# First convolution kernels wholly on VectorE, lengths and later chunks tied behind them, and sixteen products of ones ahead of the first strip

## The chip, the cores and the metric

The kernel runs on one core of a Trainium2 chip. The metric is the device time of one execution in microseconds (us), as the median of several runs. A core has five engines with a queue each: TensorE (PE in the profile, with its weight loads as PEld), VectorE (DVE), ScalarE (ACT), GpSimd (POOL) and SyncE (SP), whose queue issues most transfers here. Each engine takes its instructions strictly in the order in which the program has them, and waits on semaphores for the others.

## The reference

`x` is 128 x 32 x 512 (batch, head, position). Each head has a causal convolution kernel of 512 taps, made of 64 complex exponentials; the convolution's output is cut at each row's length, goes through a mixture of 16 experts with 4 chosen per row and one shared expert, and is added to `x`.

```python
dtA = A * dt[:, None]
Ct = Cc * (jnp.exp(dtA) - 1.0) / A
P = dtA[:, :, None] * jnp.arange(length)
K = 2.0 * jnp.einsum('hn,hnl->hl', Ct, jnp.exp(P)).real
...
y = irfft(rfft(u, n) * rfft(K, n))[..., :L] + u * D[:, None]
y = y * mask[:, None, :]            # position < length of the batch row
...
scores = sigmoid(y @ gate_w.T) + bias
topk_w, topk_idx = top_k(scores, 4) # weights divided by their sum
out = sum over chosen experts of w * (silu(y @ Wg.T) * (y @ Wu.T)) @ Wd.T
out = out + silu(y @ Sg.T) * (y @ Su.T) @ Sd.T
x = x + out
```

## The kernel before

The work runs in four stages on one core. First the **prologue** makes the first convolution kernels. Then the **convolution** handles 32 heads, four at a time (`NB` = 8 groups of `HB` = 4): for each head, `convolve` makes four products with the head's input `xt` as weights and a Toeplitz strip as moving data (512, 384, 256 and 128 columns; a float32 product is two instructions in the trace), multiplies the result by the length mask on VectorE (`yb`, L527), turns it with four transposes against the permutation `to_rank` (`pt`, L530) and copies it to `yT` (L531). `gates` and `route` compute the gate for each group and each pair of groups. Third comes the **shared expert** over all rows in eight units, and last the **chosen experts**, tile by tile, up to the end.

Convolution kernels come in chunks of pairs of heads. `CHUNKS` is `((0, 2), (2, 4), (6, 4), (10, 6))`: start and number of pairs; a pair of heads is one column of 128 partitions. For a chunk, `waves` forms angle and exponent with two interleaved chains on VectorE (the angle in `wr`, `wk`, the exponent in `wv`, `we`, `wq`, `ws`; the magnitude is `wm`), with two sines on ScalarE, and one outer product (`wv`, L309) on GpSimd. `kernels` then multiplies: the real halves (`f_r`, `ge_r`, `gg_r`, `gg_i`) on VectorE, the imaginary ones (`f_i`, `ge_i`, `gg_t`) on GpSimd. TensorE contracts them (`pk`, L394), VectorE adds the skip term (`krow`, L402), and SyncE writes the row to memory (`kd`) and reads it back as 128 shifted copies (`kernel_strip`, L419). The first chunk carries 16 further columns through the same waves for the factor `Ct` (`em`, `er`, `ei`, `nr`, `ni`, `rd`, `ct_r`, `ct_i`). Of the first group, each head's strip is a transfer of its own; of later groups, all four are one.

Between the first chunk and the loop, the program handles the lengths: keys (`key_row`, `key_col`, `num_len`, `longer`), two counting products (`rank_ps`), the permutations `to_rank` and `to_row`, then `by_rank`, `reach`, `k_u`, `unit_rows` for the shared expert, and the mask `within`. Nothing ties them to a place.

A scheduler orders each engine's queue from the program's order and its own idea of durations, so that program order and queue order differ: in the kernel before, many lengths instructions stand among those of the first chunk on VectorE, and so does the beginning of the second chunk. `chunk_at` says behind which head the later chunks are made. A manual dependence (`tc.add_manual_dep`) makes the scheduler put one instruction behind another.

Of the kernel before, what the change touches and what calls it, by code (L numbers as in the profile page):

```python
# [40 lines left out]
E, TOPK, I = 16, 4, 256  # L41
KT = L // P
IT = I // P
HB = 4
NB = H // HB
RB = 2
UB = 16
NU = B // UB
TU = UB * H
# [5 lines left out]
ONE_HOTS = 8  # L55
AHEAD = 4
# [14 lines left out]
LA, LB = 32, 16  # L71
# [4 lines left out]
def ssm_moe_kernel(  # L76
# [15 lines left out]
    nc = tc.nc  # L92
# [34 lines left out]
    nc.gpsimd.memset(dsk, 0.0)  # L127
# [21 lines left out]
    def load_xt(tb):  # L149
        t = xp.tile([P, KT, HB, P], F32, tag="x", name=f"xt{tb}")  # L150
        nc.sync.dma_start(out=t, in_=x_t[tb])
        return t

# [69 lines left out]
    nc.gpsimd.memset(run_on, 1.0)  # L223
    nc.gpsimd.memset(run_on[:, :, 0:1], 0.0)

    run_e = const.tile([P, RB * HB, E], F32, tag="run_e", name="run_e")
    nc.gpsimd.memset(run_e, 1.0)
    nc.gpsimd.memset(run_e[:, :, 0:1], 0.0)

    def floor_div(out_, in_, by):  # L230

        nc.vector.tensor_scalar(
            out_, in_, 1.0 / by, -(by - 1) / (2.0 * by), ALU.mult, ALU.add
        )
        nc.vector.tensor_scalar(out_, out_, ROUND, None, ALU.add)
        nc.vector.tensor_scalar(out_, out_, ROUND, None, ALU.subtract)

# [35 lines left out]
    CHUNKS = ((0, 2), (2, 4), (6, 4), (10, 6))  # L273
# [16 lines left out]
    nc.gpsimd.memset(f_r, 0.0)  # L290
    nc.gpsimd.memset(f_i, 0.0)
# [3 lines left out]
    def waves(c0, n, lead):  # L295


        w = lead + n * NX
        v, r, k, q = (wide(t, w) for t in ("wv", "wr", "wk", "wq"))
        s, mag = wide("ws", w, I32), wide("wm", w)  # L300

        def pairs(t):
            return t[:, lead:].rearrange("p (c x) -> p c x", x=NX)

        by_l = lab.unsqueeze(1).to_broadcast([P, n, NX])
        nc.vector.tensor_mul(
            pairs(r), by_l, dta_i[:, c0 : c0 + n].unsqueeze(2).to_broadcast([P, n, NX])
        )
        nc.gpsimd.tensor_mul(  # L309
            pairs(v), by_l, dta_r[:, c0 : c0 + n].unsqueeze(2).to_broadcast([P, n, NX])  # L310
        )
        if lead:
            nc.vector.tensor_copy(r[:, :lead], dta_i)
            nc.vector.tensor_copy(v[:, :lead], dta_r)
        reduce_angle(r, k)
        nc.vector.scalar_tensor_tensor(k, r, -1.0, r, ALU.mult, ALU.max)
        nc.scalar.activation(k, k, AF.Sin, bias=half_pi, scale=-1.0)
        half = None
        if lead:
            half = ptile("half")  # L320
# [28 lines left out]
    nc.gpsimd.tensor_mul(m0, nar, nar)  # L349
    nc.gpsimd.tensor_mul(m1, aim, aim)  # L350
    nc.gpsimd.tensor_add(m0, m0, m1)
# [15 lines left out]
    def kernels(c0, n, mag, cos, sin):  # L367

        cs = slice(c0, c0 + n)

        for j in range(2):
            rows = slice(j * N, (j + 1) * N)
            nc.vector.tensor_mul(f_r[rows, cs, j, :], cos[rows, :, LA:], mag[rows, :, LA:])
            nc.gpsimd.tensor_mul(f_i[rows, cs, j, :], sin[rows, :, LA:], mag[rows, :, LA:])
# [7 lines left out]
        nc.gpsimd.tensor_mul(e_i, sin[:, :, :LA], mag[:, :, :LA])  # L382
# [3 lines left out]
        nc.gpsimd.tensor_mul(g_t, e_i, by_i)  # L386
        nc.vector.tensor_add(g_r, g_r, g_t)
        nc.vector.tensor_mul(g_i, e_r, by_i)
        nc.gpsimd.tensor_mul(e_i, e_i, by_r)
# [12 lines left out]
        nc.vector.tensor_add(  # L402
# [7 lines left out]
        for h in range(2 * c0, 2 * (c0 + n)):  # L410
            kd_of[h] = kd[h - 2 * c0 : h - 2 * c0 + 1, :]

# [11 lines left out]

    kernels(*CHUNKS[0], *first)
    kernel_strip(0)


    len_col = const.tile([P, 1], F32, tag="len_col", name="len_col")
    nc.vector.tensor_copy(len_col, len_col_i)  # L430
    key_row = const.tile([P, B], F32, tag="key_row", name="key_row")
    nc.vector.tensor_copy(key_row, len_row_i)
    key_col = const.tile([P, 1], F32, tag="key_col", name="key_col")
    for key, raw, own in ((key_row, key_row, cpos), (key_col, len_col, ppos)):
        nc.vector.tensor_scalar(key, raw, 0.0, float(L), ALU.max, ALU.min)
        if key is key_col:
            num_len = const.tile([P, 2], F16, tag="num_len", name="num_len")
            nc.vector.tensor_copy(num_len[:, 0:1], ppos)
            nc.vector.tensor_copy(num_len[:, 1:2], key)
        nc.vector.scalar_tensor_tensor(key, key, float(P), own, ALU.mult, ALU.subtract)  # L440
# [14 lines left out]
    to_rank_h = const.tile([P, P], F16, tag="to_rank_h", name="to_rank_h")  # L455
    nc.vector.tensor_copy(to_rank_h, to_rank)

    by_rank_ps = ps_m.tile([P, 2], F32, tag="m", name="by_rank_ps")
    nc.tensor.matmul(by_rank_ps, lhsT=to_rank_h, rhs=num_len, start=True, stop=True)
    by_rank = const.tile([P, 2], F32, tag="by_rank", name="by_rank")  # L460
    nc.vector.tensor_copy(by_rank, by_rank_ps)


    reach = const.tile([P, KT], BF16, tag="reach", name="reach")
    nc.vector.memset(reach, 1.0)
    for n in range(1, KT):
        nc.vector.tensor_scalar(
            reach[:, n : n + 1], by_rank[:, 1:2], float(n * P), None, ALU.is_gt
        )

    unit = const.tile([P, NU], BF16, tag="unit", name="unit")
    nc.vector.tensor_scalar(unit, upos, 0.0, None, ALU.is_equal)
    reach_sum = const.tile([P, 1], F32, tag="reach_sum", name="reach_sum")
    nc.vector.tensor_reduce(reach_sum, reach, AX.X, ALU.add)
    reach_b = const.tile([P, 1], BF16, tag="reach_b", name="reach_b")
    nc.vector.tensor_copy(reach_b, reach_sum)
    k_u_ps = ps_m.tile([1, NU], F32, tag="m", name="k_u_ps")
    nc.tensor.matmul(k_u_ps, lhsT=reach_b, rhs=unit, start=True, stop=True)
    k_u = const.tile([1, NU], I32, tag="k_u", name="k_u")
    nc.vector.tensor_copy(k_u, k_u_ps)  # L480


    div = const.tile([P, 2], F32, tag="div", name="div")
    mod = const.tile([P, 1], F32, tag="mod", name="mod")
    floor_div(div[:, 0:1], rank, UB)
    floor_div(div[:, 1:2], ppos, UB)
    nc.vector.scalar_tensor_tensor(mod, div[:, 0:1], -float(UB), rank, ALU.mult, ALU.add)
    same_mod = const.tile([P, P], F16, tag="same_mod", name="same_mod")
    nc.vector.tensor_scalar(same_mod, pmod, mod, None, ALU.is_equal)
    row_u = const.tile([P, NU], F16, tag="row_u", name="row_u")  # L490
    nc.vector.tensor_scalar(
        row_u, cpos[:, :NU], div[:, 0:1], ppos, ALU.is_equal, ALU.mult
    )
    row_ps = ps_m.tile([P, NU], F32, tag="m", name="row_ps")
    nc.tensor.matmul(row_ps, lhsT=same_mod, rhs=row_u, start=True, stop=True)
    part = const.tile([P, TU // P], F32, tag="part", name="part")
    nc.vector.tensor_scalar(
        part, cpos[:, : TU // P], float(P // UB), div[:, 1:2], ALU.mult, ALU.add
    )
    unit_rows = const.tile([P, NU, TU // P], I32, tag="unit_rows", name="unit_rows")  # L500
    nc.vector.scalar_tensor_tensor(
        unit_rows,
        row_ps.unsqueeze(2).to_broadcast([P, NU, TU // P]),
        float(H),
        part.unsqueeze(1).to_broadcast([P, NU, TU // P]),
        ALU.mult,
        ALU.add,
    )
# [3 lines left out]
    nc.vector.tensor_scalar(within, lpos, len_col, None, ALU.is_lt)  # L512
# [337 lines left out]

    def dep(of, on, why):
        tc.add_manual_dep(of.ins, on.ins.name, SYNC, reason=why)
# [345 lines left out]
```

## Time and profile before

| what | value |
|---|---|
| time, median of 3 runs | 957.14 us (956.81 to 957.47) |
| the profiled execution | 961.51 us, of which the span is 959.8 us |
| TensorE busy | 890.6 us, 93% of the span |
| VectorE busy | 427.6 us, 45% |
| GpSimd busy | 432.0 us, 45% |
| ScalarE busy | 171.3 us, 18% |
| chain that ended last | TensorE 78%, VectorE 15%, issue 3% |
| first convolution product starts | 27.09 us |

The span runs from the first to the last instruction; the profiled execution is a single one and stands 4.4 us above the median of the other three. In the chain of waits one goes back from the last instruction to whatever released each step; a stage in which that chain is on one engine is bound by it. A start-to-start distance between two neighbouring rows of the timeline says what an instruction costs its queue, which can be less than its duration, because neighbours that do not depend on each other overlap.

### The profile page before, as it was taken

How to read it: one execution, taken by the hardware profiler on the slowest of the kernel's cores; microseconds unless marked ns; L12 is line 12 of the kernel's file. 1: busy time of each engine (PE TensorE's matmuls, PEld its weight loads, DVE VectorE, ACT ScalarE, POOL GpSimd, SP SyncE). 2: the span in 40 equal slices, each digit the busy share in tenths (PEclk: the TensorE clock that was granted, in tenths of full speed). 3: DMA queues.
4: the chain of work that ended last, by engine and by line, in shares of the span. 5: the costliest groups of instructions: out<-in, count | busy, mean ns of one | idle time of the engine just before them, and what ended most of it. 6: DMA issues, size and time to landing. Idle time of an engine off the chain costs nothing.

```text
span 959.8 us, 14544 instructions
## 1 busy us (share of the span) xinstructions
PE 890.6 (93%) x2960; PEld 443.3 (46%) x2960; DVE 427.6 (45%) x1438; ACT 171.3 (18%) x343; POOL 432.0 (45%) x400
## 2 busy tenths in 40 slices
PE   0799994989998999999999999999999999999995
PEld 0455652344444444444444444444444544444442
DVE  7955555868762233443334233423433323334332
ACT  1122221000001012221222122212222112222211
POOL 4210002033456545664556455655555445556644
PEclk9999997989999999999999999999999999999998
DMA  4467732164456676687667766766666646677755
GB/s 161 126 228 265 233 125 68 66 223 151 165 193 196 251 166 111 127 138 164 113 119 140 166 109 120 137 108 106 125 121 114 112 90 113 112 119 138 131 110 104
DMA packets 54032, 135.94 MB, mean 142 GB/s; under 512 B 12784, under 2 KB 12944, under 8 KB 51344
## 3 DMA queue, kind: packets, MB, share of 16 engines
q0 software_dynamic: 35616, 89.77, 47.5%
q1 hardware_dynamic: 14064, 36.15, 11.4%
q10 hardware_dynamic: 4224, 8.39, 2.3%
q8 instruction: 71, 1.16, 0.5%
q14 instruction: 57, 0.47, 0.1%
HBM read 288.08 MB, written 52.25 MB: 355 GB/s over the span
## 4 chain that ended last, share of the span: by engine, by line
PE 78%; DVE 15%; issue 3%; another core or an unknown queue 1%; DMA 1%; POOL 1%; ACT 0%; SPq 0%; DVEq 0%; POOLq 0%; ACTq 0%
PE g L1044 33%; PE o L1070 24%; PE m L1012 4%; PE o L930 3%; PE u L1062 3%; PE py L520 3%; PE u L904 2%; DVE cols L794 2%; PE g L904 2%; DVE rows L793 1%; DVE yb L527 1%; PE pt L530 1%; DVE wq L261 1%; PE parts L549 1%
## 5 line engine op out<-in xcount | busy, mean ns | idle before, releaser
L1044 PE MATMUL g<-store,yt 128*128 x742 | 343.1, 596 | 4.1 <-ACT yt L1018 2.7
L1080 POOL DMA_INDIRECT out<-xg,put x134 | 212.1, 1583 | 236.5 <-DVE junk L1019 203.2
L1070 PE MATMUL o<-store,zT 128*128 x536 | 252.2, 593 | 1.3 <-DVE zT L1065 1.3
L1056 DVE SCALAR_TENSOR_TENSOR zt<-g,wt,sgt 128x256 f32<-128x256 f32 x135 | 65.3, 483 | 287.0 <-ACT sgt L1055 272.6
L1044 PEld LDWEIGHTS g<-store,yt 128*128 128x128 f32 x742 | 130.3, 190 | 121.0 <-issue 116.8
L1070 PEld LDWEIGHTS o<-store,zT 128*128 128x128 f32 x536 | 101.3, 190 | 130.5 <-issue 124.3
L869 POOL DMA_INDIRECT yg<-y_rows,get x140 | 138.8, 991 | 42.8 <-issue 30.2
L1079 DVE COPY xg<-o 128x512 f32<-128x512 f32 x134 | 92.7, 692 | 110.3 <-PE o L1070 109.4
L1018 ACT COPY yt<-m 128x512 f32<-128x512 f32 x136 | 79.6, 586 | 238.1 <-PE m L1012 225.9
L1055 ACT ACTIVATE sgt<-g 128x256 f32<-128x256 f32 x135 | 51.9, 384 | 268.6 <-PE g L1044 227.8
L1012 PEld LDWEIGHTS m<-ident,yg 128*128 128x128 f32 x373 | 48.5, 141 | 73.2 <-issue 73.0
L520 PE MATMUL py<-strip,xt 128*128 128x512 f32 (+3 forms) x256 | 77.7, 443 | 5.0 <-DMA strip<-kd 5.0
L918 POOL DMA_INDIRECT xg<-in_x,unit_rows x32 | 31.1, 970 | 108.9 <-DVE sig_k L255 99.5
L939 POOL DMA_INDIRECT out<-xg,unit_rows x32 | 31.5, 984 | 98.6 <-DVE xg L937 90.4
L930 PE MATMUL o<-store,z 128*128 128x512 f32 x128 | 60.5, 622 | 6.1 <-DVE xg L937 6.1
L1012 PE MATMUL m<-ident,yg 128*128 128x128 f32 x373 | 63.3, 273 | 1.1 <-issue 1.1
L1065 DVE COPY zT<-u 128x256 f32<-128x256 f32 x134 | 56.3, 420 | 0.1
L520 PEld LDWEIGHTS py<-strip,xt 128*128 128x128 f32 x256 | 41.9, 194 | 21.8 <-issue 9.3
L1062 PE MATMUL u<-ident,zt 128*128 128x128 f32 x268 | 51.2, 273 | 0.0
L904 PE MATMUL g<-store 128*128 128x512 f32 x92 | 44.5, 621 | 0.7 <-ACT store L531 0.7
L904 PE MATMUL u<-store 128*128 128x512 f32 x92 | 42.9, 601 | 0.8 <-issue 0.8
L930 PEld LDWEIGHTS o<-store,z 128*128 128x128 f32 x128 | 24.8, 199 | 38.0 <-issue 28.0
(272 smaller groups left out, 519.7 us busy)
## 6 DMA issues: line engine op xcount, KB each, us to landing
store<-in_w_all SPq DMA_DIRECT2D x143, 1536.0 KB
xt<-in_x_t SPq DMA_DIRECT2D x8, 1024.0 KB
y_rows<-yb ACTq DMA_DIRECT2D x8, 1024.0 KB
strip<-kd SPq DMA_DIRECT2D x7, 1024.0 KB
yg<-y_rows,get POOLq DMA_INDIRECT x140
out<-xg,put POOLq DMA_INDIRECT x134
strip<-kd SPq DMA_DIRECT2D x4, 256.0 KB
xg<-in_x,unit_rows POOLq DMA_INDIRECT x32
```

The costliest lines, as they stand in the source:

```text
L520: nc.tensor.matmul(py[:, : L - jt * P], lhsT=xt[:, jt, q, :], rhs=strip[tb][:, q, jt * P :], start=(jt == 0), stop=(jt == KT - 1),)
L869: nc.gpsimd.indirect_dma_start(out=at(yg, t), out_offset=None, in_=y_rows[:, :], in_offset=bass.IndirectOffsetOnAxis(ap=made["get"][:, t : ...
L904: nc.tensor.matmul(ps[it], lhsT=w_sh[:, c0 : c0 + P], rhs=yT[:, u, kt, :, :].rearrange("p h b -> p (h b)"), start=(kt == KT - n), stop=(kt ...
L930: nc.tensor.matmul(po, lhsT=at(zu, u)[:, it, q * P : (q + 1) * P], rhs=w_sh[:, c0 : c0 + L], start=(it == 0), stop=(it == IT - 1),)
L1012: nc.tensor.transpose(pt[:, q, :], at(yg, t)[:, q * P : (q + 1) * P], ident)
L1018: nc.scalar.copy(at(yt, t), pt)
L1044: mm = nc.tensor.matmul(pgu, lhsT=at(yt, t)[:, q, :], rhs=ring_flat[:, bass.ds(w0s[t] + q * 2 * I, 2 * I)], start=(q == KT - n), stop=(q = ...
L1056: nc.vector.scalar_tensor_tensor(at(zs, t), pgu[:, I:], at(wts, t), sg, ALU.mult, ALU.mult)
L1062: nc.tensor.transpose(at(p_z, t)[:, it, :], at(zs, t)[:, it * P : (it + 1) * P], ident)
L1070: mm = nc.tensor.matmul(po, lhsT=at(zts, t)[:, it, :], rhs=ring_flat[:, bass.ds(w0s[t] + WD + it * L, L)], start=(it == 0), stop=(it == IT ...
L1079: nc.vector.tensor_copy(ob, po)
L1080: add = nc.gpsimd.indirect_dma_start(out=out, out_offset=bass.IndirectOffsetOnAxis(ap=put[:, t : t + 1], axis=0), in_=ob, in_offset=None, ...
```

## The change

Seven memory fills move from GpSimd to VectorE (`dsk`, two of `run_on`, two of `run_e`, `f_r`, `f_i`). In the first chunk all that GpSimd did goes to VectorE (`wv`, `m0`, `m1`, `f_i`, `ge_i`, `gg_t`). A new `behind` ties instructions behind the first chunk's `krow` addition: the lengths' first ones, `within`, and the first products of each later chunk. What the shared expert needs of the lengths moves into a function `ranks`, called before the third group of heads. The chunks become 2, 2, 4 and 8 pairs, the last one made behind head 7 instead of head 5. `keep_warm` adds sixteen products of a 128 x 128 matrix of ones with itself, repeated to 512 columns; nothing reads their result.

```diff
-    nc.gpsimd.memset(dsk, 0.0)
+    nc.vector.memset(dsk, 0.0)
...
-    nc.gpsimd.memset(run_on, 1.0)
-    nc.gpsimd.memset(run_on[:, :, 0:1], 0.0)
+    nc.vector.memset(run_on, 1.0)
+    nc.vector.memset(run_on[:, :, 0:1], 0.0)
...
-    nc.gpsimd.memset(run_e, 1.0)
-    nc.gpsimd.memset(run_e[:, :, 0:1], 0.0)
+    nc.vector.memset(run_e, 1.0)
+    nc.vector.memset(run_e[:, :, 0:1], 0.0)
...
-    CHUNKS = ((0, 2), (2, 4), (6, 4), (10, 6))
+    CHUNKS = ((0, 2), (2, 2), (4, 4), (8, 8))
...
-    nc.gpsimd.memset(f_r, 0.0)
-    nc.gpsimd.memset(f_i, 0.0)
+    nc.vector.memset(f_r, 0.0)
+    nc.vector.memset(f_i, 0.0)
...
-        nc.vector.tensor_mul(
+        first_op = nc.vector.tensor_mul(
             pairs(r), by_l, dta_i[:, c0 : c0 + n].unsqueeze(2).to_broadcast([P, n, NX])
         )
-        nc.gpsimd.tensor_mul(
+        if c0:
+            behind(first_op)
+        first_op = (nc.gpsimd if c0 else nc.vector).tensor_mul(
             pairs(v), by_l, dta_r[:, c0 : c0 + n].unsqueeze(2).to_broadcast([P, n, NX])
         )
+        if c0:
+            behind(first_op)
...
-    nc.gpsimd.tensor_mul(m0, nar, nar)
-    nc.gpsimd.tensor_mul(m1, aim, aim)
-    nc.gpsimd.tensor_add(m0, m0, m1)
+    nc.vector.tensor_mul(m0, nar, nar)
+    nc.vector.tensor_mul(m1, aim, aim)
+    nc.vector.tensor_add(m0, m0, m1)
...
+        other = nc.gpsimd if c0 else nc.vector
...
-            nc.gpsimd.tensor_mul(f_i[rows, cs, j, :], sin[rows, :, LA:], mag[rows, :, LA:])
+            other.tensor_mul(f_i[rows, cs, j, :], sin[rows, :, LA:], mag[rows, :, LA:])
...
-        nc.gpsimd.tensor_mul(e_i, sin[:, :, :LA], mag[:, :, :LA])
+        other.tensor_mul(e_i, sin[:, :, :LA], mag[:, :, :LA])
...
-        nc.gpsimd.tensor_mul(g_t, e_i, by_i)
+        other.tensor_mul(g_t, e_i, by_i)
...
-        nc.gpsimd.tensor_mul(e_i, e_i, by_r)
+        other.tensor_mul(e_i, e_i, by_r)
...
-        nc.vector.tensor_add(
+        last = nc.vector.tensor_add(
             krow,
...
+        return last
...
-    kernels(*CHUNKS[0], *first)
+    def keep_warm(on):
+        warm = ps_u.tile([P, KT, P], F32, tag="u", name="warm")
+        for n in range(WARM):
+            mm = nc.tensor.matmul(
+                warm,
+                lhsT=ones,
+                rhs=ones.unsqueeze(1).to_broadcast([P, KT, P]),
+                start=True,
+                stop=True,
+            )
+            dep(mm, on, "behind the first kernels")
+
+    chunk0 = kernels(*CHUNKS[0], *first)
     kernel_strip(0)
+    keep_warm(chunk0)
+
+    def behind(op):
+
+        dep(op, chunk0, "later in VectorE's order")
...
-    nc.vector.tensor_copy(len_col, len_col_i)
+    behind(nc.vector.tensor_copy(len_col, len_col_i))
...
-    nc.vector.tensor_copy(key_row, len_row_i)
+    behind(nc.vector.tensor_copy(key_row, len_row_i))
...
-            nc.vector.tensor_copy(num_len[:, 0:1], ppos)
+            behind(nc.vector.tensor_copy(num_len[:, 0:1], ppos))
...
+    def ranks():
+
+        to_rank_h = const.tile([P, P], F16, tag="to_rank_h", name="to_rank_h")
...
+        behind(nc.vector.tensor_scalar(unit, upos, 0.0, None, ALU.is_equal))
...
+        behind(floor_div(div[:, 1:2], ppos, UB))
...
+        return by_rank, reach, k_u, unit_rows
...
-    nc.vector.tensor_scalar(within, lpos, len_col, None, ALU.is_lt)
+    behind(nc.vector.tensor_scalar(within, lpos, len_col, None, ALU.is_lt))
...
-    chunk_at = {0: CHUNKS[1], 2: CHUNKS[2], HB + 1: CHUNKS[3]}
+    chunk_at = {0: CHUNKS[1], 2: CHUNKS[2], 2 * HB - 1: CHUNKS[3]}
     for tb in range(NB):
+        if tb == 2:
+            by_rank, reach, k_u, unit_rows = ranks()
```

In the queues as built, VectorE has the seven fills first, then the first chunk without a break up to `krow`, then ten lengths instructions, then the second chunk. On TensorE the sixteen products stand between the first chunk's `pk` and `rank_ps`, and the second chunk's `pk` between the products of heads 0 and 1. On SyncE, three small `kd<-zero` transfers, which stood ahead of the first `kd<-krow`, now stand between it and the four strips. The first `k_u` load of TensorE, early in the queue before, now stands at the end of the convolution.

More of the change, by code (lines that the diff above doesn't have):

```diff
@@ L55 @@
 ONE_HOTS = 8
+WARM = 16
 AHEAD = 4
@@ L152, in load_xt, with dep @@
         return t
+    def dep(of, on, why):
+        tc.add_manual_dep(of.ins, on.ins.name, SYNC, reason=why)
     ident = const.tile([P, P], F32, tag="ident", name="ident")
@@ L222, in ssm_moe_kernel @@
     run_on = const.tile([P, E, H], F32, tag="run_on", name="run_on")
-    nc.gpsimd.memset(run_on, 1.0)
-    nc.gpsimd.memset(run_on[:, :, 0:1], 0.0)
+    nc.vector.memset(run_on, 1.0)
+    nc.vector.memset(run_on[:, :, 0:1], 0.0)
     run_e = const.tile([P, RB * HB, E], F32, tag="run_e", name="run_e")
-    nc.gpsimd.memset(run_e, 1.0)
-    nc.gpsimd.memset(run_e[:, :, 0:1], 0.0)
+    nc.vector.memset(run_e, 1.0)
+    nc.vector.memset(run_e[:, :, 0:1], 0.0)
     def floor_div(out_, in_, by):
-        nc.vector.tensor_scalar(
+        first_op = nc.vector.tensor_scalar(
             out_, in_, 1.0 / by, -(by - 1) / (2.0 * by), ALU.mult, ALU.add
@@ L236, in floor_div @@
         nc.vector.tensor_scalar(out_, out_, ROUND, None, ALU.subtract)
+        return first_op
     def ptile(name):
@@ L454, in ssm_moe_kernel @@
     nc.vector.tensor_scalar(to_row, rank_ps[:, :B], ppos, None, ALU.is_equal)
[L455 to L464, printed above, removed]
@@ L465, in ssm_moe_kernel @@
-    nc.vector.memset(reach, 1.0)
-    for n in range(1, KT):
+    def ranks():
+        to_rank_h = const.tile([P, P], F16, tag="to_rank_h", name="to_rank_h")
+        nc.vector.tensor_copy(to_rank_h, to_rank)
+        by_rank_ps = ps_m.tile([P, 2], F32, tag="m", name="by_rank_ps")
+        nc.tensor.matmul(by_rank_ps, lhsT=to_rank_h, rhs=num_len, start=True, stop=True)
+        by_rank = const.tile([P, 2], F32, tag="by_rank", name="by_rank")
+        nc.vector.tensor_copy(by_rank, by_rank_ps)
+        reach = const.tile([P, KT], BF16, tag="reach", name="reach")
+        nc.vector.memset(reach, 1.0)
+        for n in range(1, KT):
+            nc.vector.tensor_scalar(
+                reach[:, n : n + 1], by_rank[:, 1:2], float(n * P), None, ALU.is_gt
+            )
+        unit = const.tile([P, NU], BF16, tag="unit", name="unit")
+        behind(nc.vector.tensor_scalar(unit, upos, 0.0, None, ALU.is_equal))
+        reach_sum = const.tile([P, 1], F32, tag="reach_sum", name="reach_sum")
+        nc.vector.tensor_reduce(reach_sum, reach, AX.X, ALU.add)
+        reach_b = const.tile([P, 1], BF16, tag="reach_b", name="reach_b")
+        nc.vector.tensor_copy(reach_b, reach_sum)
+        k_u_ps = ps_m.tile([1, NU], F32, tag="m", name="k_u_ps")
+        nc.tensor.matmul(k_u_ps, lhsT=reach_b, rhs=unit, start=True, stop=True)
+        k_u = const.tile([1, NU], I32, tag="k_u", name="k_u")
+        nc.vector.tensor_copy(k_u, k_u_ps)
+        div = const.tile([P, 2], F32, tag="div", name="div")
+        mod = const.tile([P, 1], F32, tag="mod", name="mod")
+        floor_div(div[:, 0:1], rank, UB)
+        behind(floor_div(div[:, 1:2], ppos, UB))
+        nc.vector.scalar_tensor_tensor(mod, div[:, 0:1], -float(UB), rank, ALU.mult, ALU.add)
+        same_mod = const.tile([P, P], F16, tag="same_mod", name="same_mod")
+        nc.vector.tensor_scalar(same_mod, pmod, mod, None, ALU.is_equal)
+        row_u = const.tile([P, NU], F16, tag="row_u", name="row_u")
@@ L467, in ssm_moe_kernel @@
         nc.vector.tensor_scalar(
-            reach[:, n : n + 1], by_rank[:, 1:2], float(n * P), None, ALU.is_gt
+            row_u, cpos[:, :NU], div[:, 0:1], ppos, ALU.is_equal, ALU.mult
         )
[L471 to L508, printed above, removed]
+        row_ps = ps_m.tile([P, NU], F32, tag="m", name="row_ps")
@@ new lines, in ranks @@
+        nc.tensor.matmul(row_ps, lhsT=same_mod, rhs=row_u, start=True, stop=True)
+        part = const.tile([P, TU // P], F32, tag="part", name="part")
+        nc.vector.tensor_scalar(
+            part, cpos[:, : TU // P], float(P // UB), div[:, 1:2], ALU.mult, ALU.add
+        )
+        unit_rows = const.tile([P, NU, TU // P], I32, tag="unit_rows", name="unit_rows")
+        nc.vector.scalar_tensor_tensor(
+            unit_rows,
+            row_ps.unsqueeze(2).to_broadcast([P, NU, TU // P]),
+            float(H),
+            part.unsqueeze(1).to_broadcast([P, NU, TU // P]),
+            ALU.mult,
+            ALU.add,
+        )
@@ L849, in ssm_moe_kernel @@
     fp = ctx.enter_context(tc.tile_pool(name="fp", bufs=2))
-    def dep(of, on, why):
-        tc.add_manual_dep(of.ins, on.ins.name, SYNC, reason=why)
     def load_expert(e, dst, cond=None):
```

## The prediction

> **What bounds it now.** I read the busy shares first, then the chain of waits, then single stages.
>
> ```profile
> PE 890.6 (93%) x2960; PEld 443.3 (46%) x2960; DVE 427.6 (45%) x1438; ACT 171.3 (18%) x343; POOL 432.0 (45%) x400
> ...
> PE   0799994989998999999999999999999999999995
> ...
> DVE  7955555868762233443334233423433323334332
> ```
>
> TensorE bounds the span; in slice 0 it does nothing and VectorE works. That stage, by windows (columns: stretch, length, then busy time of PE, PEld, DVE, ACT and POOL, the granted clock, the DMA share, GB/s):
>
> ```profile
> 0.00:22.18 22.18, 1.70 (x13) 1.00 (x13) 17.36 (x111) 2.07 (x4) 9.74 (x44) 1.00 0.48 173
> 22.18:27.09 4.91, 0.00 (x0) 0.00 (x1) 4.28 (x16) 0.71 (x2) 0.66 (x2) 1.00 0.40 118
> 27.09:58.40 31.31, 27.65 (x165) 17.26 (x166) 25.51 (x75) 6.27 (x12) 7.77 (x17) 1.00 0.48 152
> ...
> 66.10:139.52 73.42, 71.89 (x361) 44.25 (x359) 42.48 (x148) 16.34 (x30) 0.00 (x0) 1.00 0.62 206
> ```
>
> Until 27.09 TensorE waits for the first strip; to 58.4 VectorE, making later chunks, holds it up; from about 54 TensorE is never free. The chain there shows a head at 2.16 us of products and 0.63 of transposes, 2.8 in all. What starts earlier before 54 shifts the rest. The timeline of the first stage (start, duration, instruction):
>
> ```profile
> 5.05 0.51 POOL L223 MEMSET run_on<- 128x512 f32 x1
> ...
> 5.15 1.62 DVE L263 TENSOR_SCALAR dn_s<-dn_k 128x32 int32<-128x32 f32 x1
> ...
> 6.21 0.51 POOL L291 MEMSET f_i<- 128x512 f32 x1
> ...
> 6.83 0.18 DVE L259 TENSOR_SCALAR dn_q<-logs 128x32 f32<-128x32 f32 x1
> ...
> 22.41 0.32 SPq L409 DMA_DIRECT2D kd<-krow  x1
> ...
> 23.82 1.76 SPq L419 DMA_DIRECT2D strip<-kd  x4
> ...
> 27.09 3.95 PE L520 MATMUL py<-strip,xt 128*128 128x512 f32 x8 [4.95 <-DMA strip<-kd]
> ```
>
> **Fills.** The conversion at L263 takes 1.62 us where the same on four times the columns (`sig_s`) takes 0.22, and ends as the fills on GpSimd end. [...] Without it L259 would start at 5.49, 1.34 earlier. [...] the row at 4.58 beside GpSimd's fills took a normal 0.21. I take the row, 1.34; if it has another cause, 0. The fills on VectorE cost four times about 0.5 (the row of `within`, 512 columns, is 0.47) and some 0.4 for the small ones: from 0.89 to 3.3, under the wait for `logs` that ends at 4.12. If they ran to 4.6, the cost would be 0.5.
>
> **First chunk on VectorE**, by start-to-start distances (a 16-wide step 0.09 to a neighbour, 0.21 to a dependent; 112 wide 0.13 to 0.19 and 0.31):
> - to the first angle step (L244, now 10.43): less 1.34; less ten lengths steps of 0.06 to 0.39, sum 1.50; plus `m0`, `m1`, their sum, `rd` and `wv`, 0.8. It starts at 8.4.
> - to `wm` (now 16.09, so 5.66): some twenty lengths steps go. Left are 13 interleaved steps, 2.04, and six chained products of 0.30: 3.85, to 12.25. ScalarE's sines end by 11.4 and hide.
> - to `krow` (now 22.18, so 6.09): the second chunk's beginning goes (eight steps of 0.17 to 0.35, near 2.0), with two waits for GpSimd (0.37) and collisions (`t` L332 took 0.49, not 0.17); six multiplications come, 0.6. About 4.45, so `krow` at 16.7. Gain 5.5; from 3.5 (stall stays, more dependents) to 6.
>
> **Transfers.** Three `kd<-zero` now follow `kd<-krow` on SyncE: 1.21 by their row. Before, the first strip went out 1.41 after `krow`'s transfer, 0.32 of them issue, so they end 0.1 late. At 16.9 the queue still carries the last megabyte of `xt` until 17.7 (the DMA share falls there from 0.98 to 0.05), behind which `krow` stands: the strip goes out near 18.7, between 18.5 and 20. With 3.27 from issue to product it is there at 22.0.
>
> **Products of ones.** The first head took 3.95 us for 8 products, a later one 2.35, since the clock was still low; that the clock column says 1.00 there means only that it saw no change. Later it shows one:
>
> ```profile
> 160.00:164.00 4.00, 1.97 (x5) 0.50 0.12 45
> 164.00:168.00 4.00, 4.00 (x8) 0.66 0.16 16
> ...
> 200.00:204.00 4.00, 4.00 (x11) 0.89 0.54 216
> ```
>
> After idling, the full clock came 4.7 us after the restart at 162.03, 6.1 after that at 194.76, and about 3.3 after 27.09. [...] That speaks against a fixed number of products: too few leave the clock low, too many keep the strip waiting. A f16 product of 143 columns costs 0.0625 (eight in 0.50), so 512 columns 0.22, twice that cold. With the clock up after f, sixteen take 3.5 + f/2: 5.1 by the first row (f = 3.3)[...]. I take f = 4.9, between the rows: 5.9. From 16.95 they end at 22.85, `rank_ps` 0.3 later: head 0 starts at 23.2, not 22.0, and runs 2.35 to 25.55, not 31.0. The cover for late strips is 1.2.
>
> **After `krow`: chunks and heads.** VectorE does ten lengths steps (1.7), then the second chunk, 96 wide, `wm` near 22.3, ranks (0.6; `rank_ps` is just there). GpSimd's `wv`, `f_i`, `ge_i`, `gg_t`, `ge_i` (0.69, 0.57, 0.35, 0.35, 0.33) end near 24.75; `gg_i` at 25.05 releases `pk`, which stands ahead of head 1. Head 1 starts near 26.1, not 31.59. `within` and `to_rank` are ready.
>
> The new ties: on VectorE they order a queue and wait for nothing. On GpSimd the second chunk's `wv` waits for `krow`; behind it stand only later chunks' steps, which wait for VectorE anyway. On TensorE the products of ones wait for `krow`; behind them stand `rank_ps` and head 0, which the sum above has. On SyncE the third chunk's `kd<-krow` stands behind an `xt` that waits for head 3's products, near 35; `krow` itself comes at 37.8.
>
> The chunks' total is unchanged: 96 + 192 + 384 columns of 672, as 192 + 192 + 288. From `krow` to the last `gg_i` VectorE took 29.5 (22.26 to 51.73) with five `yb`. After: the 2.0 that stood ahead of `krow`, 3.0 of lengths, three more `yb` (1.8): 36.3, from 16.7 to 53, with 1 of waiting 54. By the same walk TensorE has done heads 0 to 8 and the first product of head 9 then; now, at 53.3, heads 0 to 5 and the first of head 6. Three heads of 2.8 are 8.4; less 0.8 later, less 0.3 for eight more `pk` (32 for 24): 7.3. The walk on to head 10, from 54.1: `pk` 1.1, transposes 0.63, gate `parts` 1.06, products 0.75, gate `pg` 0.96 with a short wait, products 0.75; 59.4, where the same work is done at 66.1 now. That is 6.7. I take it, being the longer walk, and 0.4 off for the clock's phase, which the first row had at its shortest: **6.3**. Strips are not late: that of heads 4 to 7 lands near 32, wanted at 34.6; the next at 44, wanted at 50.
>
> **Moved and hidden.** `ranks` costs VectorE 2 us, part of it in gaps of dependent steps, and TensorE three small products (0.2 each) in head 14; the wait for `cw` there stays 12.5 us behind the gate. Cost 0 to 0.5, 0.3 inside the walk's rounding. `k_u`'s load lies under the wait for the last `yb`, 0.88 in the trace; uncovered up to 0.5. Later waits (11.9 us for `cw` at 151 to 162, the `xg` transfer at 321) hang on earlier steps and shift along.
>
> **Sum.** The profiled execution, 961.51 (span 959.8), becomes 955.2; its place above the other runs is no part of the change, so on the median 957.14 less 6.3 is 950.8.
>
> **Rivals.**
> - VectorE still holds TensorE (0.17). For: `ge_r` took 0.58 at 27.91 and `gg_r` 0.48 where 0.28 is normal beside GpSimd, three chunks long; 384-wide steps stand ahead of `yb`. If the last `gg_i` comes at 57, the gain is 3.4: 953.7. Against: the same rows were in the stretch I counted.
> - The first strip lags (0.06): `krow` waits behind `xt` and the zeros, head 0 at 25.5. With 1.2 of cover lost and VectorE's stretch as the limit after it, gain 4.3: 952.8.
> - TensorE waits for nothing after 26.1 (0.12): 9 heads at 2.8, `pk` and gates of 6 bring head 10 at 57.3, gain 8.8: 948.3. Against: VectorE is full to 54.
> - VectorE becomes the bound (0.05): its stretch of 36.3 has to grow by 6.7, or 18%, to eat the gain[...]. At 25% it is 9.1: 959.5.
> - Given back or without effect (0.05): the scheduler had already hidden the lengths; 957.1. Against: L244 to `wm` took 5.66 for 3.85 of work.
> - The forecast: 0.55, from 949 to 952.7.
>
> A change of 0.2% (1.9 us) is about what can be told from none. Faster: 0.55 + 0.17 + 0.06 + 0.12 less 0.01, 0.89; same 0.06, slower 0.05. The range 948.0 to 954.5 leaves out the last two rivals and little else.
>
> **What would show it.** Right: L263's like near 0.2; `krow` at 16 to 17.5; first product at 22 to 24, the first head in 2.4; head 1 by 26.5; the last chunk's `pk` near 54 within head 9. Wrong: TensorE idle between heads 0 and 5 for over 3 us; the first head still near 4 us; the end of the convolution (138.0 is its last `yb`) less than 4 us earlier.

## The result, and the profile after

| what | before | after |
|---|---|---|
| median, us | 956.97 (956.22 to 957.47, 4 runs) | 950.09 (949.70 to 950.25, 4 runs) |
| the profiled execution: time, span | 961.51, 959.8 | 950.25, 948.4 |
| first product of a head starts | 27.09 | 23.01 |
| transposes of the last head start | 138.86 | 132.14 |

The ratio is 0.9928, with a 95% interval from 0.9911 to 0.9945: 6.88 us faster between the medians, where 6.3 was forecast. The two spans differ by more, 11.4 us, because the profiled execution of the kernel before stood 4.5 above its other runs; that part is not the change's. The clean measure in the trace is the end of the convolution: 138.86 to 132.14, 6.72 us.

The page of the changed kernel, busy shares and the VectorE and TensorE rows of the forty slices:

```profile
PE 892.1 (94%) x2976; PEld 444.7 (47%) x2976; DVE 429.9 (45%) x1454; ACT 171.1 (18%) x343; POOL 427.5 (45%) x384
...
PE   3999984899999999999999999999999999999995
...
DVE  8984535967852333433334334423333233344332
```

TensorE has 16 instructions more (the products of ones), and its first two slices read 3 and 9 where they read 0 and 7; VectorE, which makes the first kernels, is fuller in slice 0. The timeline of the changed kernel, one line for each step that the prediction named (start, duration, instruction; in brackets the idle time before it and what ended it):

```profile
4.97 0.17 DVE L268 TENSOR_SCALAR dn_s<-dn_k 128x32 int32<-128x32 f32 x1
...
16.92 0.21 DVE L412 TENSOR_TENSOR krow<-pk,dsk 32x64 f32<-32x64 f32 x1 [0.62 <-PE pk L404]
...
17.28 5.82 PE L440 MATMUL warm<-ones 128*128 128x512 bf16 x16 [0.40 <-DVE krow L412]
...
18.99 1.76 SPq L430 DMA_DIRECT2D strip<-kd  x4
...
23.01 2.37 PE L553 MATMUL py<-strip,xt 128*128 128x512 f32 x8
...
36.56 0.25 PE L404 MATMUL pk<-f_r,gg_r 128*32 128x32 f32 x2 [1.83 <-DVE gg_r L397]
...
53.63 0.41 DVE L400 TENSOR_TENSOR gg_i<-gg_i,ge_i 128x256 f32<-128x256 f32 x1
...
53.76 0.25 PE L404 MATMUL pk<-f_r,gg_r 128*32 128x32 f32 x2 [0.89 <-DVE gg_r L397]
```

The 1.62 us conversion is 0.17, `krow` comes 5.26 earlier than before (22.18), the first head takes 2.37 instead of 3.95, and two waits for VectorE's chunks are left ahead of `pk`.

To read where 6.72 us come from, take the stretch from the first product to the last head's transposes, which holds nearly the same work in every kernel here (three small rank products lie inside it after and ahead of it before), and split its length into what TensorE was busy and the rest. In the windows view (columns as in the prediction) it is this row before:

```profile
27.09:138.86 111.77, 106.57 (x554) 64.97 (x555) 70.07 (x226) 24.36 (x45) 7.77 (x17) 1.00 0.59 195
```

and this one after:

```profile
23.01:132.14 109.13, 104.35 (x561) 64.57 (x559) 74.41 (x244) 24.25 (x45) 8.08 (x16) 1.00 0.60 197
```

Three terms: the stretch starts 4.08 earlier; TensorE is busy 2.22 less; and it idles 111.77 - 106.57 = 5.20 before and 4.78 after, 0.42 less. Together 6.72. Of the 2.22, the eight products of head 0 give 3.95 - 2.37 = 1.58, since they no longer run at the low clock. The other 0.64 lies behind head 0, where the clock is full in both kernels, and which instructions give it was not traced. The granted-clock column says 1.00 in both rows, so the low clock at the start is seen in the durations. The trace's record of the clock agrees with them: it has its first entry, the full clock, at 30.20 before, 3.1 into head 0, and at 21.77 after, ahead of head 0.

### The profile page after: what moved, and what is told of

It reads as the page before. It is cut to its first block, busy times and chain, and to the rows that moved or that the text cites. A ratio compares the mean times of both kernels' runs of the same rounds, so it can differ in the third digit from the quotient of the medians.

```text
span 948.4 us, 14566 instructions
## 1 busy us (share of the span) xinstructions
PE 892.1 (94%) x2976; PEld 444.7 (47%) x2976; DVE 429.9 (45%) x1454; ACT 171.1 (18%) x343; POOL 427.5 (45%) x384
## 3 DMA queue, kind: packets, MB, share of 16 engines
q1 hardware_dynamic: 14064, 36.15, 11.4%
## 4 chain that ended last, share of the span: by engine, by line
PE 83%; DVE 13%; issue 2%; SPq 1%; POOL 0%; ACT 0%; DMA 0%; POOLq 0%; DVEq 0%; ACTq 0%
PE g L1076 34%; PE o L1102 24%; PE o L962 5%; PE m L1044 4%; PE u L936 4%; PE u L1094 3%; PE g L936 3%; PE py L553 3%; DVE cols L827 2%; DVE yb L560 1%; DVE rows L826 1%; PE pt L563 1%; PE parts L582 1%; DVE sig_q L266 1%; PE pg L593 1%
```

## The experiments

Two theories stand against each other. **VectorE theory** (the prediction's walk): VectorE's queue, up to the last chunk's `gg_i` near 54, sets where TensorE stands, so what counts is what VectorE has to do ahead of each chunk. **Clock theory**: the gain is mostly the first head at the full clock. Apart from its repetition and the last two, each run changes one part of the changed kernel. They ran on three chips, in three groups; each is compared with runs of the kernel before on its own chip (956.77, 962.34 and 957.23 us). The four terms are from each run's own profile, in the manner just shown:

| run | first product | TensorE busy | idle | last transposes | against 132.14 | median | ratio to before (95% interval) |
|---|---|---|---|---|---|---|---|
| changed kernel | 23.01 | 104.35 | 4.78 | 132.14 | | 950.09 | 0.9928 (0.9911 to 0.9945) |
| no_ones | 22.37 | 107.55 | 4.99 | 134.91 | +2.77 | 952.74 | 0.9961 (0.9948 to 0.9975) |
| fills_back | 24.22 | 104.33 | 4.40 | 132.95 | +0.81 | 952.14 | 0.9955 (0.9941 to 0.9968) |
| gpsimd_first | 23.59 | 104.88 | 5.27 | 133.74 | +1.60 | 951.91 | 0.9950 (0.9936 to 0.9964) |
| untied | 26.48 | 104.18 | 3.37 | 134.03 | +1.89 | 952.09 | 0.9949 (0.9935 to 0.9963) |
| after_again | 23.49 | 104.53 | 4.56 | 132.58 | +0.44 | 956.03 | 0.9937 (0.9924 to 0.9951) |
| chunks_back | 22.93 | 107.05 | 6.54 | 136.52 | +4.38 | 959.15 | 0.9972 (0.9961 to 0.9983) |
| ranks_early | 22.77 | 104.84 | 5.63 | 133.24 | +1.10 | 955.21 | 0.9927 (0.9914 to 0.9941) |
| waves_tied | 22.70 | 104.81 | 3.93 | 131.44 | -0.70 | 954.28 | 0.9917 (0.9904 to 0.9931) |
| warm4 | 22.19 | 108.74 | 4.48 | 135.41 | +3.27 | 953.42 | 0.9955 (0.9941 to 0.9968) |
| warm12 | 22.27 | 107.06 | 6.00 | 135.33 | +3.19 | 953.45 | 0.9959 (0.9945 to 0.9972) |
| both | 22.61 | 105.14 | 5.81 | 133.56 | +1.42 | 953.07 | 0.9958 (0.9944 to 0.9971) |
| both9 | 22.57 | 105.45 | 5.54 | 133.56 | +1.42 | 952.79 | 0.9954 (0.9940 to 0.9967) |

The end of the convolution tells runs apart to some 0.4 us (the two profiles of the changed kernel differ by 0.44), the medians to one or two: what follows the convolution adds up to 1.5 either way. By the ratios alone, only chunks_back lies clear of both measurements of the changed kernel, and no_ones of the first; every other interval overlaps with it or touches it, so that what is said of those runs rests on one profile each. The first product moves with the clock's phase as well, the time from TensorE's start or restart to the full clock: sixteen products of ones took from 4.82 (waves_tied) to 6.35 us (gpsimd_first), 5.82 and 6.26 in the two profiles of the changed kernel itself, as the full clock came 2.5 to 5.6 after the first of them.

### Without the products of ones

```diff
-    keep_warm(chunk0)
```

> The change without its sixteen products of ones. Theory (VectorE's queue up to the last chunk sets the gain): the first strip is there at 22.3 us, head 0 takes about 3.9 us for 2.37 and ends near 26.2 instead of 25.4; the second chunk's contraction, ready at 25.4, is then behind it, and TensorE's later waits (1.8 us near 35, 0.9 near 53) take up most of it: last mask multiplication at 131.3 to 132.1, time 950.1 to 950.9 us. Rival (the clock makes the gain): the clock stays low over more than one head and the loss is 1.6 us or more: 951.7 us and above.

Measured: `krow` unmoved at 16.95, first product 0.64 earlier at 22.37, end of the convolution 2.77 later, 952.74 us.

```profile
22.37 4.51 PE L552 MATMUL py<-strip,xt 128*128 128x512 f32 x8 [3.14 <-DMA strip<-kd]
```

Head 0 takes 4.51 us for the same eight products, with the strip's wait in the brackets. The busy time rises by 3.20 (107.55 to 104.35), 2.14 of it in this row; in the trace's record the clock is full from 26.61, so the other 1.06 is not the clock and is not placed. The clock's own share of the 6.72 is thus 1.58 (head 0 before and after), and 2.14 in this run. The loss at the end is more than the VectorE theory allowed, which had VectorE's work absorb it. The rival had the number and not the way: the clock is full again within head 0. VectorE does not absorb the loss: its `yb` multiplications wait in its queue for head 0, it is busy 2.63 us of the four from 23 to 27 instead of 3.76, and the third chunk's `gg_r` also comes 1.97 later (37.99 for 36.02). The queue changed too: three of the four steps of the second chunk's `pk` now stand behind a head's transposes, its `krow` comes at 28.89 instead of 26.47, and TensorE waits 0.58 for the next strip at 36.13. How much of the 2.77 is this order and how much the clock, the run does not tell apart.

### The fills back on GpSimd

```diff
-    nc.vector.memset(run_on, 1.0)
+    nc.gpsimd.memset(run_on, 1.0)
...
-    nc.vector.memset(f_r, 0.0)
-    nc.vector.memset(f_i, 0.0)
+    nc.gpsimd.memset(f_r, 0.0)
+    nc.gpsimd.memset(f_i, 0.0)
```

> The change with its seven fills back on GpSimd. Theory: the conversion dn_s again takes about 1.6 us, until the fills end near 6.7; krow comes 1.3 us later, at 18.2, and head 0 at 24.3; time 951.4 us. Rival (the long conversion had another cause, or VectorE has time to spare): dn_s stays near 0.2 us, or krow is late and nothing else; time 950.1 us.

Measured: `krow` at 18.32, 1.40 later; end of the convolution 0.81 later. The timeline of this run, VectorE and GpSimd:

```profile
5.14 0.50 DVE L268 TENSOR_SCALAR dn_s<-dn_k 128x32 int32<-128x32 f32 x1
...
5.71 1.14 DVE L264 TENSOR_SCALAR dn_q<-logs 128x32 f32<-128x32 f32 x1
...
5.79 0.51 POOL L295 MEMSET f_r<- 128x512 f32 x1
...
6.29 0.51 POOL L296 MEMSET f_i<- 128x512 f32 x1
```

The conversion itself takes 0.50 here. But the next instruction but one, 0.18 in the changed kernel, takes 1.14 and ends at 6.85, as the last 512-wide fill on GpSimd ends at 6.80; before, the conversion ended at 6.77 and that fill at 6.72. `dn` is 1.34 later, which is the very number of the prediction. So the stall belongs to the fills and not to the conversion: in both kernels it struck what VectorE had in hand beside them. It was not every instruction: the one at 4.57, beside smaller work of GpSimd, took a normal 0.21.

### The first chunk's multiplications back on GpSimd

```diff
-        other = nc.gpsimd if c0 else nc.vector
+        other = nc.gpsimd
```

(with `wv`, `m0`, `m1` and their sum in the same way)

> The change with the first chunk's multiplications on GpSimd as before (outer product, m0, m1, their sum, f_i, ge_i, gg_t). Theory: VectorE has nine steps fewer, near 1.2 us by start-to-start distances, but waits for GpSimd (0.4) and collides with it (0.8): krow within 0.4 us of 16.9, time 949.7 to 950.5 us. Rival (keeping GpSimd at rest is the heart of the change): krow 2 us later or more, time 952 us or more.

Measured: `krow` at 17.05, only 0.13 later. The end of the convolution, though, is 1.60 later: the ones reach the full clock later, the first product comes 0.58 later, TensorE is busy 0.53 more, and 0.49 more of waits follow. The later start cannot be put down to this part, since the changed kernel's second profile has it too (23.49). What GpSimd did in the first chunk was almost wholly beside VectorE's own steps; of the change's title, "wholly on VectorE" is the part that gives least at `krow`.

### Without the ties

```diff
 def behind(op):
-    dep(op, chunk0, "later in VectorE's order")
+    return op
```

> The change without its ties: lengths and second chunk may stand among the first chunk on VectorE again (ranks stays in the third group, the fills and the first chunk on VectorE, the products of ones stay). Krow should come 2.5 us later, near 19.4. Theory A (krow's time sets the gain): everything is 2.5 us later, 952.6 us. Theory B (VectorE's total work up to the last chunk sets it, since TensorE waits for VectorE at the second and third chunk anyway): what stands ahead of krow is missing behind it, the last chunk ends at 54 as before, TensorE's waits near 35 and 53 shrink, and the time is 950.1 to 950.7 us.

Measured: `krow` 2.97 later at 19.89, first product 3.47 later at 26.48, 0.37 of it because the second chunk's `pk` here stands ahead of it; yet the end of the convolution comes only 1.89 later. The third chunk's `pk` on TensorE, and the windows row:

```profile
35.31 0.25 PE L404 MATMUL pk<-f_r,gg_r 128*32 128x32 f32 x2 [0.44 <-DVE gg_r L397]
```

```profile
26.50:134.03 107.53, 104.16 (x551) 64.44 (x550) 69.94 (x221) 24.14 (x45) 6.54 (x11) 1.00 0.61 198
```

TensorE idles 107.53 - 104.16 = 3.37 here against 4.78. VectorE has done the lengths, the permutations and part of the second chunk before `krow`, so it is ahead afterwards: the wait ahead of the third chunk's `pk` falls from 1.83 to 0.44, the one ahead of the last is gone, and the last `krow` comes at 53.89 instead of 55.27. This is what the VectorE theory says: its total is the same, so a later start is partly given back. The result falls between what the two theories expected, as both limits act.

### The changed kernel once more, and the chunks as before

> The changed kernel itself once more, as the measure for the runs beside it on the same chip, and for the four before. Both theories: 949.5 to 950.6 us, last yb of the convolution at 131.3 (130.9 to 131.7) in its profile.

On this chip both kernels are some 5 to 6 us slower (962.34 and 956.03); their distance, 6.31, is the same. Its last `yb` came at 131.7.

```diff
-    CHUNKS = ((0, 2), (2, 2), (4, 4), (8, 8))
+    CHUNKS = ((0, 2), (2, 4), (6, 4), (10, 6))
...
-    chunk_at = {0: CHUNKS[1], 2: CHUNKS[2], 2 * HB - 1: CHUNKS[3]}
+    chunk_at = {0: CHUNKS[1], 2: CHUNKS[2], HB + 1: CHUNKS[3]}
```

> Only the four chunks go back to pairs 0-1, 2-5, 6-9, 10-15, the last one behind head 5. VectorE theory (while TensorE is at the first heads, VectorE's wave steps for the next chunk end last): the second chunk's gg_i comes some 2 us later (192 wide for 96, 17 steps that each take 0.09 to 0.13 us more), so head 1 or 2 waits; the waits at the third chunk and at the last shrink. Last yb 0.5 to 2 us later, 950.6 to 952. Clock theory (the 2.4 us head and the end of the restart are the gain, the chunks only fill VectorE's idle time): within 0.3 us of the kernel as changed, 949.8 to 950.4.

Measured: last `yb` at 135.7, 4.0 later than in the run beside it and twice what the VectorE theory allowed; 3.1 us by the medians. The second chunk's `krow` comes at 31.10 (26.89 in the run beside it). Its row goes to memory and back as the strip of heads 4 to 7, which is now late (issued at 32.93; at 28.53 in the run beside it). The timeline of TensorE in this run, then its windows:

```profile
36.45 0.63 PE L563 MATMUL pt<-to_rank,yb 128*128 128x128 f32 x4 [0.91 <-DVE yb L560]
38.58 1.97 PE L553 MATMUL py<-strip,xt 128*128 128x512 f32 x2 [1.50 <-DMA strip<-kd]
```

```profile
36.00:38.00 2.00, 0.63 (x4) 0.42 (x4) 1.44 (x6) 0.59 (x1) 1.27 (x3) 1.00 1.16 340
38.00:40.00 2.00, 1.42 (x2) 0.43 (x2) 1.97 (x7) 0.00 (x0) 1.76 (x4) 0.67 0.96 282
40.00:42.00 2.00, 2.00 (x18) 1.43 (x18) 2.00 (x8) 0.00 (x0) 0.18 (x1) 0.50 0.93 348
42.00:44.00 2.00, 2.00 (x12) 0.54 (x11) 2.00 (x8) 0.27 (x1) 0.00 (x0) 0.98 1.05 400
```

Read the clock column, third from the right: after the two waits of 0.91 and 1.50 it falls to 0.5 at about 38.66 and returns at 42.07. In these 3.41 us TensorE does half the work, 1.7 us lost; that is why the two instructions at 38.58 take 1.97 where 1.10 is normal. So the small second chunk buys two things: an early strip, and no second loss of the clock. The prediction had the order of the chunks only as a sum of columns on VectorE.

### The ranks ahead of the loop

```diff
+    by_rank, reach, k_u, unit_rows = ranks()
     for tb in range(NB):
-        if tb == 2:
-            by_rank, reach, k_u, unit_rows = ranks()
```

> Only the rank steps behind to_row go back ahead of the heads in the program's order. VectorE theory: they come to some 25 narrow instructions, 3 to 4 us of VectorE, of which what falls ahead of the second chunk's gg_i delays it; last yb 0.3 to 1.5 us later, 950.4 to 951.6. Rival (the scheduler places them in VectorE's gaps in either order, as my forecast's 0 to 0.5): within 0.4 us, 949.8 to 950.5.

The last `yb` came at 132.4, 0.7 later than in the run beside it, and the median is 0.8 faster, with intervals that overlap. No effect that could be told from none.

### An addition: the last chunk's opening tied behind the third chunk

```diff
+        if c0 == CHUNKS[3][0]:
+            dep(first_op, prior[0], "behind the chunk before")
```

(behind both opening multiplications in `waves`; `prior` holds what `kernels` returned last)

> An addition to the changed kernel: the two multiplications that open the last chunk's waves wait for the third chunk's krow too, so that GpSimd's 1.14 us one no longer stands ahead of the third chunk's f_i, nor VectorE's 0.55 us one ahead of its gg_r. VectorE theory: TensorE's 1.83 us wait ahead of the third chunk's pk shrinks to some 0.3 to 0.8; the last chunk's steps begin later by as much as they now overlap, so the wait of 0.89 ahead of its pk stays or grows to 1.5; last yb 0.4 to 1.5 us earlier, 948.7 to 949.8. Rival (the last chunk's steps set the pace from 37 us on, so that what is won at the third chunk is lost at the last): within 0.3 us, 949.8 to 950.4.

In the changed kernel GpSimd has the last chunk's 384-wide `wv` (1.14 us) at 32.53, ahead of the third chunk's `f_i`, which comes at 33.63. Here the third chunk goes first:

```profile
32.89 0.75 POOL L390 TENSOR_TENSOR f_i<-wr,wm 64x64 f32<-64x64 f32 x2 [7.94 <-DVE wm L340]
...
36.78 0.83 POOL L320 TENSOR_TENSOR wv<-lab,dta_r 128x384 f32<-128x384 f32 x1 [1.40 <-DVE krow L418]
```

```profile
35.17 0.25 PE L410 MATMUL pk<-f_r,gg_r 128*32 128x32 f32 x2 [0.68 <-DVE gg_r L403]
35.76 0.25 PE L410 MATMUL pk<-f_i,gg_i 128*32 128x32 f32 x2 [0.34 <-DVE gg_i L406]
```

TensorE's wait falls from 1.83 to 0.68 and 0.34, the last `yb` comes at 130.6, 1.1 earlier than in the run beside it. But 0.79 of this 1.14 is the earlier first product (22.70 for 23.49), as the ones took 4.82 here and 6.26 there, which is the clock's phase; the waits give 0.63, and 0.28 more of busy time takes part of it back. The median is 1.75 lower, but the intervals of the two ratios overlap and the fastest run of the changed kernel there (953.20) lies below all of these (953.80 to 954.65). The wait is shown to shrink as expected; that the kernel is faster is likely and not established.

### Fewer products of ones

```diff
-WARM = 16
+WARM = 4
```

> Only the number of products of ones goes from 16 to 4, so that TensorE stands idle for some 3 us again before the strip lands. Clock theory (it is the clock at the strip's landing that the products buy): as without them, head 0 takes 4.2 to 4.6 us instead of 2.4, last yb 1.5 to 3 us later, 951.5 to 953.2 on a chip where the kernel as changed takes 950.1. Rival (the products bring the expected order on VectorE, or the first stretch of them is enough): head 0 below 3 us, within 0.5 us of the kernel as changed.

```diff
-WARM = 16
+WARM = 12
```

> Only the number of products of ones goes from 16 to 12: the last four, 0.21 us each at the full clock, stand between the strip's landing and head 0. Clock theory: the clock is up by the tenth product, the twelfth ends near 22.3, head 0 begins 0.4 to 0.8 us earlier at its 2.4 us; last yb 0 to 0.7 us earlier, 949.5 to 950.2 on a chip where the kernel as changed takes 950.1. Rival (the clock needs the longer run, or the strip lands at 23 in any case): head 0 at 23.0 or half cold, 3 to 4 us long, last yb 0.3 to 1.5 later.

With 4, the first ten products take 5.11 us, the end of the convolution comes 3.27 later: the clock theory's side, and a little more than it expected, as 1.7 of it is another loss of the clock, from 39.55 to 42.96. With 12 the expectation failed. Head 0 does start 0.74 earlier, at 22.27, at the full clock, and the end is 3.19 *later*. TensorE and the windows of that run:

```profile
26.78 0.66 PE L563 MATMUL pt<-to_rank,yb 128*128 128x128 f32 x4 [0.52 <-DVE yb L560]
27.36 0.25 PE L404 MATMUL pk<-f_r,gg_r 128*32 128x32 f32 x2
...
37.09 0.25 PE L404 MATMUL pk<-f_r,gg_r 128*32 128x32 f32 x2 [2.73 <-DVE gg_r L397]
```

```profile
37.00:39.00 2.00, 1.91 (x5) 0.46 (x5) 1.92 (x7) 0.00 (x0) 0.00 (x0) 0.65 0.77 313
39.00:41.00 2.00, 2.00 (x20) 1.94 (x20) 1.02 (x4) 0.00 (x0) 0.00 (x0) 0.50 1.02 375
41.00:43.00 2.00, 2.00 (x8) 1.27 (x8) 1.52 (x3) 0.59 (x1) 0.00 (x0) 1.00 0.40 121
```

The scheduler placed the queues differently for four products less. `rank_ps` stands behind the ones on TensorE, so it comes at 21.5 instead of 22.9, and VectorE gets the rank steps ahead of the second chunk's last ones. On TensorE a head's transposes, which wait 0.52 for `yb`, now stand in the middle of the second chunk's `pk`, and its `krow` comes at 27.71 instead of 26.47. The third chunk is 0.5 later, while TensorE is there 0.4 earlier: the wait grows from 1.83 to 2.73, and after it the clock falls, from 37.61 to 41.02. A head start of 0.74 turned into a loss of 1.2 by waiting, and 2.7 of busy time, 1.7 of it by the clock. The other 1.0 I can't place; the order of the queues is likely to have a part in it, since the run both, below, has transposes in the same place and kept the clock, and is also busy 0.79 more.

> The last chunk's opening multiplications tied behind the third chunk's krow, and 12 products of ones. If the two gains stand in different waits they add up: last yb 1.1 to 1.8 us before that of the kernel as changed, ratio to the kernel before 0.9905 to 0.992. If what the earlier head 0 wins is waited for again at the third chunk's pk: as with the tie alone, last yb 0.8 to 1.2 earlier, ratio 0.991 to 0.9925.

> As the run with tie and 12 products, and the last chunk behind head 9 instead of 7. VectorE theory: the steps of the last chunk stand 5 us later against TensorE's heads, so its pk no longer waits (0.9 to 1.5 us of wait go), last yb 0.5 to 1.2 us before the one with both. Rival (its steps follow data, not the place in the program, or two chunks' parts collide elsewhere): within 0.4 us of the one with both.

Neither adds up. With the tie and 12 products the end is 1.42 later than in the changed kernel: transposes stand ahead of half of the second `pk` here too, the wait at the third chunk is 1.60 and 0.33, but the clock holds. With the last chunk behind head 9 its `krow` moves from 55.43 to 61.14 and nothing is gained (133.56 in both). None of the versions is established as faster than the changed kernel.

## Why the prediction was right

- **Fills.** 1.34 forecast for the stall. `dn` is 1.34 earlier than with the fills on GpSimd, and `krow` 1.40. One row of the kernel before was thus the right measure. The row at 4.58, a normal 0.21, stood beside smaller work of GpSimd: the first 512-wide fill there starts at 5.05.
- **First chunk to `krow`.** 5.5 forecast, 5.26 measured; the angle step started at 8.18 (8.4), `wm` at 12.03 (12.25), `krow` at 16.92 (16.7). By undoing one part each, ties give 2.97, fills 1.40, the multiplications 0.13; that leaves 0.8 which shows only with them together. The sum charged the moved multiplications some 1.4 (0.8 and 0.6) against 0.7 of waits and collisions saved; taken back, they make `krow` 0.13 later, so they came free. One leg was mis-sized. From `wm` to `krow` the terms listed add up to 4.0 and not to the 4.45 that was written, and 4.89 was measured; 0.62 of it is VectorE waiting for `pk` (the row at 16.92), a gap that the second chunk's steps filled before, so that taking those steps away saved nothing.
- **Transfers and ones.** The strip went out at 18.99 (18.7) and was there near 22.2 (22.0; the runs in which TensorE waits for it do so until 22.19 to 22.77). The ones ended near 23.1 after 5.82 us (5.9), head 0 began at 23.01 (23.2) and took 2.37 (2.35). That the ones came so close is luck: the rise of the clock was taken at 4.9 and came 4.5 after the first of them, but 5.4 in the second profile of the changed kernel and as little as 2.5 in waves_tied, below the shortest of the prediction's rows (about 3.3). The cover for a late strip was some 0.75 here (18.99 and 3.27 give 22.26) and not 1.2, and where the clock came early (ranks_early, waves_tied) it was used up, with 0.32 and 0.51 of wait for the strip.
- **The walk to 54.** The last `gg_i` ended at 54.04 (54) with TensorE within head 9 (head 9), and the end of the convolution moved by 6.72 (6.7). It holds in its parts too: head 0 was to end at 25.55 instead of 31.0, 5.5 earlier, and ended at 25.38 instead of 31.04, 5.66 earlier. What the walk left for the stretch behind it, 1.2, came out as 1.06: 0.64 less busy time and only 0.42 less waiting. Neither theory holds alone: most of the gain is the earlier start (4.08), then the clock (1.58). The undone parts add up to 0.81 + 1.60 + 1.89 + 2.77 + 3.94 = 11.0 us (the last against the run beside it) against 6.72 for all: each part covers for others, and the chunks' sizes, to which I gave no term of their own, cost most when taken back, through a late strip and the clock.
- **The clock's phase.** Here the sign was wrong: 0.4 was taken off, and the profile shows 0.4 to the good. After the restart at 155.32 the full clock took 6.4 us (4.7 before), which cost 0.85; after that at 188.89 it took 3.55 (6.1 before), which brought 1.27. At `pa` the changed kernel leads by 211.14 - 204.00 = 7.14. This is the phase of single executions, so the 0.6 between forecast and median should not be called explained by it.
- **Ranks and ties.** 0 to 0.5 forecast for the ranks, not told from nothing. The ties were costed at nothing as waits, rightly; that on VectorE they give half of their gain back (3.47 at the first product, 1.89 at the end) the sum did not show apart.

Of the rivals, "VectorE holds TensorE" was half true: 2.7 us of such waits are left, but the last `gg_i` came at 54 and not at 57.

## What to carry to other kernels

Where two engines feed each other, split a stretch into its start, its busy time and its idle time before and after a change: start alone misleads, as a head start of 0.74 us here ended in a loss of 3.2, and a start 3.47 late in one of only 1.89. A wait of TensorE has two prices, its own length and, where the clock falls after it as in chunks_back, warm4 and warm12, 1.7 us more (3.41 us at half the clock). And where a scheduler orders the queues, taking one part away also moves others, so parts undone one at a time need not add up.

## What the hardware did that I had not expected

- The clock fell in the middle of the convolution without any long rest: after a single wait of 2.73 us in warm12, after waits of 0.91 and 1.50 with work between them in chunks_back, and, in warm4, after 0.30 and 1.53. Each time it came back 3.41 us later (37.61 to 41.02, 38.66 to 42.07, 39.55 to 42.96). It did not fall after one of 1.83 in the changed kernel nor 1.97 in gpsimd_first. So no single length of wait decides. In the traces of both kernels the changes of the clock lie whole multiples of 3.41 apart (36, 4, 8, 2 and 220 of them before; 36, 5, 8, 1 and 220 after), and in warm12 the falls at 37.61 and 146.83 lie 32 apart, so stretches of 3.41 can be laid out from any one change. Here is the stretch ahead of the fall in warm12 and in warm4, and the emptiest stretch between 23 and 60 us of the changed kernel and of the run both, which kept the clock (TensorE's busy time is the third number):

```profile
34.19:37.60 3.41, 0.68 (x5) 0.43 (x4) 2.97 (x9) 0.14 (x1) 2.39 (x6) 1.00 0.60 221
36.13:39.54 3.41, 1.82 (x22) 1.08 (x21) 2.99 (x10) 0.00 (x0) 1.76 (x3) 1.00 0.84 310
35.42:38.83 3.41, 2.27 (x23) 1.64 (x24) 3.28 (x11) 0.00 (x1) 0.86 (x2) 1.00 0.83 331
35.26:38.67 3.41, 1.85 (x19) 1.17 (x20) 2.60 (x7) 0.00 (x0) 1.85 (x4) 1.00 0.74 259
```

  The waits lie differently in these stretches: the 0.30 of warm4 ended at 35.62, ahead of its stretch, the 1.83 wait of the changed kernel (34.73 to 36.56) is cut in two by the border at 35.42, while the 2.73 of warm12 (34.36 to 37.09) lies within one. That this place counts is my reading of these rows and not shown. Nor does the busy time of a stretch settle it: the clock fell in warm4 with 1.82 of 3.41 busy and held in the run both with 1.85 and in the changed kernel with 2.27, but elsewhere it fell after a stretch with 2.41 busy (warm12, 143.42 to 146.83).
- Fills on GpSimd, which read nothing, held back VectorE instructions of 32 columns for up to 1.4 us (1.62 for 0.17 in the kernel before, 1.14 for 0.18 in fills_back); both ended 0.05 after the last 512-wide fill.
- One chip ran both kernels some 5 us slower than the other two, with the distance between the kernels kept (6.31 and 6.88).
